# Two attention blocks on one core: transposes into eight PSUM banks by row chunks, image 0's norm inside the first product of weights, bias vectors as rows

## The chip, the core and the metric

The kernel runs on one core of a Trainium2 chip. The core has five engines that run side by side, each with its own queue of instructions in a fixed order: TensorE (PE) multiplies matrices and loads the stationary operand (PEld), VectorE (DVE), ScalarE (ACT) and GpSimd (POOL) work element by element, and SyncE (SP) issues most of the transfers between the chip's memory (DRAM) and the core's working memory. Engines wait for each other through semaphores. TensorE writes its results into PSUM, eight banks of 128 partitions by 512 fp32 numbers, from which DVE or ACT copy them out. The metric is the device time of one execution in microseconds (us). Before the change it is 3001.4 us, the median of 3 runs (2998.86 to 3006.32).

## The reference

The input is 8 images of 512 channels and 32 x 32 points, in fp32. Two attention blocks follow each other; everything is fp32.

```
# layer 0: group norm with 32 groups, 8 heads of 64 channels
h   = group_norm(x, 32 groups)
qkv = w_qkv @ h + b_qkv
att = softmax(q.T k / sqrt(64))            # 1024 x 1024 for each head
x   = x + w_proj @ (v @ att.T) + b_proj
# layer 1: group norm with 8 groups, one head of 512 channels
h = group_norm(x, 8 groups)
q, k, v = q_w @ h + q_b, k_w @ h + k_b, v_w @ h + v_b
att = softmax(q.T k / sqrt(512))
x = x + p_w @ (v @ att.T) + p_b
```

## The kernel before, in words

**What is computed.** The kernel folds layer 1's weights in pairs. Scores need only the product of the q and k weights (called m), and values followed by the projection need only the product of the p and v weights (called z). Both 512 x 512 products are made on the chip in a prologue, and so are the three vectors that come from biases carried through a weight matrix: `ubias`, `obias[1]` and `obias[0]`. A multiplication of an image by a weight matrix is done with seven products of half-sized blocks instead of eight (`wino`, L223). For that each weight matrix needs four sums of its quarters; `prepare` (L273) loads the quarters and makes the sums in four DVE instructions, and `keep` (L285) stores the seven blocks (1.8 MB) to DRAM, from where `load_weight` (L293) fetches them again whenever an image needs them. Three such weight tiles fit at a time, so the load of one waits until an earlier one has been stored or used.

**The prologue** (L554). It loads the raw k and q weights of layer 1 and image 0 and prepares v, q and k of layer 0. `natural` (L519) transposes a weight matrix, 16 blocks of 128 x 128 for each matrix, into PSUM, four blocks to a bank, and copies each bank out, even ones on DVE and odd ones on ACT. `product` (L532) multiplies, four outputs with four accumulating matmuls each. An fp32 matmul is two records in the profile, a transpose is one. `GroupNorm` (L88) has three parts: `stats` on DVE, `group_mean` (a small matmul and four small DVE instructions) and `affine` (a small matmul, DVE, a power on POOL, DVE), after which `apply` scales each of the four 128-channel chunks, in the prologue in turn on POOL and ACT. `bias_product` (L542) multiplies with the weights as the stationary operand and one bias column as the moving one. Then come the v, q and k products of image 0, the second product of weights (z), the other two bias vectors, and the norm of image 1. `acc_tile` (L187) gives one of two PSUM banks; three more pools (a, b, c) have two banks each.

**The attention of layer 0** (`attention0`, L395) works in 8 blocks for an image: a pair of heads by one half of the points. For each of 8 steps PE makes a score tile `sc` of two banks (three such tiles exist), ACT takes its exponential `e`, and DVE adds it to `total`. PE then multiplies the exponentials with v (`av`) and, in `reciprocals` (L366), adds `total` over partitions (the `sums` matmul). DVE takes the reciprocal (`rc`), SP writes it to DRAM as rows and reads it back to all partitions as `r`, and one block later DVE multiplies, `a <- av, r` (L435). Functions in `extra` are called inside the blocks: for image 0 they hold what `later` collected in the prologue (L594 to L598), that is the sums, the store and a weight load for p, m and z, in blocks 0, 1 and 2, and the norm of image 1.

**What sets the order.** A scheduling layer places instructions in each engine's queue by its own estimates, within the dependencies it sees. Instructions handed to `tc.keep_in_program_order` keep the order of the program among each other. Before the change that was so only for matmuls and transposes (L65 to L69); so the sums of weights could run on DVE much earlier than where the program names them.

## Time and profile before

The profile's execution has a span of 2998.6 us. All of the change lies in the first 150 us and in the first attention blocks.

| event | time, us |
| --- | --- |
| first transpose of the k weights | 4.9 |
| first product of weights on PE | 19.2 to 34.8 |
| small matmuls of ubias and image 0's norm | 34.6 to 39.5 |
| v, q and k products of image 0 | 42.8 to 117.1 |
| transposes of the v weights | 117.0 to 120.0 |
| second product of weights | 120.0 to 134.0 |
| bias matmuls of obias | 134.4 to 145.3 |
| first score matmul, first exponential | 145.3, 147.4 |
| sums of p, m, z on DVE begin | 73.9, 87.6, 145.4 |
| `sums` matmuls of the first five blocks | 162.1, 176.7, 191.9, 206.5, 222.4 |

The columns of a timeline line in what follows are: start, duration, engine, line of the kernel, operation, written tile and tiles read, shapes, how many such instructions were merged, and in brackets the time that the engine stood idle before it and what ended that. SPq is SP's queue, where a transfer has the time of its issue, not of its data. In the lines of stretches, each engine has its busy time and its number of instructions; the three last numbers are the clock that PE was granted (1.00 is full speed), the busy share of the 16 transfer engines and the GB/s that they moved. Busy time says little of what ends last; what counts is the idle time before an instruction on PE.

### The profile page before, as it was taken

The page shows a single profiled execution, that of the slowest core. Times are in us where ns is not written, and L with a number is a line of the kernel's source. Part 1 is how long each engine was busy: PE and PEld are TensorE (multiplying, and loading weights), DVE is VectorE, ACT ScalarE, POOL GpSimd, SP SyncE. Part 2 cuts the span into 40 slices and gives each one's busy share as a digit, 9 for nine tenths or more (in the row PEclk, how much of TensorE's full clock was granted, in tenths as well). Part 3 has the DMA queues.
Part 4 walks back from the last instruction along what each step waited for, and adds up shares of the span by engine and source line. Part 5 has one row for each costly group of instructions (what it writes and reads, how often), then busy time and mean ns, then how long its engine had stood idle before and what let it go on. Part 6 is the DMA issues. An engine that isn't in the chain of part 4 may idle for free.

```text
span 2998.6 us, 26895 instructions
## 1 busy us (share of the span) xinstructions
PE 2944.2 (98%) x10322; PEld 1409.5 (47%) x10322; DVE 1836.1 (61%) x2445; ACT 754.6 (25%) x925; POOL 112.8 (4%) x119
## 2 busy tenths in 40 slices
PE   7999999999999999999999999999999999999899
PEld 5535454354543545435453354534445354543345
DVE  4376565764667647575466754677546765557745
ACT  1153111421124111341114411143111431214220
POOL 0000000000000000000000000000000000000000
PEclk9999999999999999999999999999999999999899
DMA  7422314023140231402322133411324023030100
GB/s 258 166 80 80 138 60 172 19 92 130 59 169 18 107 142 51 150 27 100 144 101 96 47 115 113 145 46 46 130 105 168 19 76 140 33 144 19 39 0 37
DMA packets 78296, 283.56 MB, mean 95 GB/s; under 512 B 9360, under 2 KB 16336, under 8 KB 71632
## 3 DMA queue, kind: packets, MB, share of 16 engines
q1 hardware_dynamic: 77744, 281.61, 26.3%
q8 instruction: 83, 1.36, 0.2%
q14 instruction: 53, 0.43, 0.0%
q10 hardware_dynamic: 416, 0.16, 0.0%
HBM read 207.51 MB, written 74.22 MB: 94 GB/s over the span
## 4 chain that ended last, share of the span: by engine, by line
PE 84%; DVE 7%; issue 4%; DMA 3%; ACT 1%; SPq 0%; POOL 0%; DVEq 0%; ACTq 0%; POOLq 0%
PE sc L66 9%; PE av L66 8%; PE psb_av L66 5%; PE psb_sc L66 5%; DVE sum L417 5%; PE psa_av L66 4%; PE psc_av L66 4%; PE psc_sc L66 4%; PE psa_sc L66 4%; PE psb_z L66 3%; PE psb_q L66 3%; PE psb_v L66 3%; PE psb_g L66 3%; PE psb_k L66 3%; PE psb_p L66 2%
## 5 line engine op out<-in xcount | busy, mean ns | idle before, releaser
L413 ACT ACTIVATE e<-sc 128x1024 f32<-128x1024 f32 x512 | 476.4, 1051 | 582.7 <-PE sc L66 582.7
L417 DVE TENSOR_TENSOR sum<-sum,e 128x1024 f32<-128x1024 f32 x384 | 469.8, 1223 | 34.5 <-ACT e L413 0.8
L66 PE MATMUL sc<-q_again,k_again 64*128 64x512 f32 x1792 | 399.7, 596 | 0.0
L66 PE MATMUL av<-e,v_again 128*64 128x512 f32 x1792 | 396.9, 595 | 0.0
L66 PEld LDWEIGHTS sc<-q_again,k_again 64*128 64x128 f32 x1792 | 166.7, 186 | 212.2 <-ACT e L413 103.7
L66 PEld LDWEIGHTS av<-e,v_again 128*64 128x64 f32 x1792 | 123.7, 137 | 266.3 <-issue 254.2
L377 DVE RECIPROCAL rc<-sums 128x256 f32<-128x256 f32 x72 | 126.4, 1756 | 80.3 <-PE sums L66 47.7
L379 POOL TENSOR_TENSOR all_recs<-all_recs,rc 128x256 f32<-128x256 f32 x72 | 63.6, 883 | 1611.1 <-DVE rc L377 1611.1
L464 ACT ACTIVATE e<-e 128x512 f32<-128x512 f32 x96 | 60.3, 630 | 238.8 <-DVE e L463 238.8
L66 PE MATMUL psa_sc<-g,h 128*128 128x512 f32 x256 | 115.1, 592 | 0.0
L66 PE MATMUL psa_av<-e,z 128*128 128x512 f32 x256 | 113.2, 595 | 0.0
L415 DVE TENSOR_TENSOR sum<-e,e 128x1024 f32<-128x1024 f32 x64 | 78.4, 1225 | 48.9 <-ACT e L413 48.9
L136 ACT ACTIVATE h<-h,b,s 128x1024 f32<-128x1024 f32 x30 | 36.5, 1238 | 169.3 <-DMA h<-in_x 161.4
L66 PEld LDWEIGHTS psa_sc<-g,h 128*128 128x128 f32 x256 | 48.6, 190 | 61.2 <-issue 61.2
L66 PEld LDWEIGHTS psa_av<-e,z 128*128 128x128 f32 x256 | 48.0, 190 | 54.8 <-issue 50.6
L435 DVE TENSOR_TENSOR a<-av,r 128x512 f32<-128x512 f32 x64 | 43.9, 686 | 46.2 <-DMA r<-rows 46.2
L234 DVE TENSOR_TENSOR u_av<-psb_av,t_av 128x512 f32<-128x512 f32 x16 | 11.1, 691 | 93.1 <-PE psb_av L66 93.1
L66 PE MATMUL psb_p<-t_a,w_p 128*128 128x512 f32 x128 | 60.5, 615 | 5.2 <-DVE t_a L167 5.2
L66 PE MATMUL sums<-sum,ones 128*32 128x256 f32 x576 | 46.0, 391 | 18.1 <-DVE sum L417 17.9
L66 PE MATMUL psa_g<-h,w_m 128*128 128x512 f32 x128 | 60.0, 613 | 3.2 <-ACT h L136 3.2
L66 PE MATMUL sc<-q,k 64*128 64x512 f32 x256 | 59.2, 612 | 0.7 <-ACT e L413 0.7
L66 PE MATMUL psb_z<-w_z,t_h 128*128 128x256 f32 x256 | 58.4, 381 | 0.0
(281 smaller groups left out, 4159.1 us busy)
## 6 DMA issues: line engine op xcount, KB each, us to landing
x<-in_x SPq DMA_DIRECT2D x36, 512.0 KB
h<-in_x SPq DMA_DIRECT2D x32, 512.0 KB
r<-rows SPq DMA_DIRECT2D x128, 128.0 KB
out<-x SPq DMA_DIRECT2D x64, 256.0 KB
w_p<-sums_p SPq DMA_DIRECT2D x8, 1792.0 KB
spill<-v SPq DMA_DIRECT2D x28, 512.0 KB
w_m<-sums_m SPq DMA_DIRECT2D x8, 1792.0 KB
spill<-q SPq DMA_DIRECT2D x28, 512.0 KB
```

What stands on the lines that cost most here:

```text
L66: tc.keep_in_program_order(nc.tensor.matmul(*args, **kw))
L136: nc.scalar.activation(dst, src, AF.Identity, bias=b, scale=s)
L234: nc.vector.tensor_add(t[i], ps["b", i], t1[i])
L377: nc.vector.reciprocal(rc, sums)
L379: nc.gpsimd.tensor_tensor(all_recs, all_recs, rc, ALU.add)
L413: nc.scalar.activation(e, sc, AF.Exp, scale=(C // 8) ** -0.5)
L415: nc.vector.tensor_add(total, es[0], e)
L417: nc.vector.tensor_add(total, total, e)
L435: nc.vector.tensor_mul(a[hp][:, ts(tb, HT)], av, r)
L464: nc.scalar.activation(dst, dst, AF.Exp, scale=scale)
```

## The change

It rebuilds the prologue so that PE has less to wait for, in these parts:

- `raw` loads a weight matrix in four row chunks instead of two halves. `natural` goes through the chunks in its outer loop, so that a chunk is transposed as soon as it has landed, into four banks at once. The k and q weights together use all eight banks.
- The copies of transposed weights (DVE and ACT in turn), the statistics of image 0 and the sums of weights are kept in program order. The sums of v now stand after the first product.
- `group_mean` and `affine` of image 0 are called inside the first product, after its seventh and tenth matmul, and `apply` follows there.
- `bias_product` gives way to `bias_products`: a bias column is the stationary operand, the weights are the moving one, and the three results lie in one bank as rows at partitions 0, 32 and 64. They are copied out, written to DRAM as rows and read back as columns. All three are made after the second product.
- The raw weights for `obias[0]` are loaded before the second product.

```diff
--- before.py
+++ after.py
@@ -86,15 +86,17 @@
 
 
     class GroupNorm:
-        def __init__(self, layer, uid):
-            self.layer, self.uid = layer, uid
+        def __init__(self, layer, uid, pinned=False):
+            self.layer, self.uid, self.pinned = layer, uid, pinned
             self.mv = small.tile([P, KC, 2], F32, tag="mv", name=f"mv_{uid}")
             self.st = [None] * KC
 
         def half_stats(self, c, half, xh):
             if self.st[c] is None:
                 self.st[c] = small.tile([P, 2, 6], F32, tag="bnst", bufs=4, name=f"bnst_{self.uid}_{c}")
-            nc.vector.bn_stats(self.st[c][:, half, :], xh)
+            stats = nc.vector.bn_stats(self.st[c][:, half, :], xh)
+            if self.pinned:
+                tc.keep_in_program_order(stats)
 
         def end_stats(self, c):
             nc.vector.bn_aggr(self.mv[:, c, :], self.st[c])
@@ -278,7 +280,8 @@
                 nc.sync.dma_start(f[p], half(kh, mh))
             _, steps = left_sums(
                 [(f[1], f[7])], [(f[2], f[4])], (lambda j: f[5], lambda j: f[6], lambda j: f[3]),
-                nc.vector.tensor_add, nc.vector.tensor_sub,
+                lambda *a: tc.keep_in_program_order(nc.vector.tensor_add(*a)),
+                lambda *a: tc.keep_in_program_order(nc.vector.tensor_sub(*a)),
             )
             return t, steps
 
@@ -511,67 +514,86 @@
 
         def raw(n, i):
             ts_ = [pair_tile(f"raw{n}_{h}") for h in range(2)]
-            for h in range(2):
-                nc.sync.dma_start(ts_[h], w[i, ts(h, C // 2), :].rearrange("(kc p) o -> p kc o", p=P))
+            for kc in range(KC):
+                nc.sync.dma_start(ts_[kc // 2][:, kc % 2, :], w[i, ts(kc, P), :])
             return [ts_[kc // 2][:, kc % 2, :] for kc in range(KC)]
 
-
-        def natural(wt, nm):
+        def ps_tile(n, name):
+            return acc_tile(name) if n == "acc" else ps_pools["abc".index(n)].tile([P, HT], F32, tag="ps", name=name)
+
+        def spread(f, n):
+
+            for i in range(n):
+                f(i, nc.scalar.copy if i % 2 else nc.vector.tensor_copy)
+
+
+        def natural(wt, nm, banks):
             ts_ = [pair_tile(f"nat{nm}_{h}") for h in range(2)]
             t = [ts_[o // 2][:, o % 2, :] for o in range(KC)]
-            for o in range(KC):
-                pt = acc_tile(f"tr_w{nm}_{o}")
-                for kc in range(KC):
-                    transpose(pt[:, ts(kc, P)], wt[kc][:, ts(o, P)], ident)
-                if o % 2 == 0:
-                    nc.vector.tensor_copy(t[o], pt)
-                else:
-                    nc.scalar.copy(t[o], pt)
+            pt = [ps_tile(banks[o // 2], f"tr_w{nm}_{o}") for o in range(KC)]
+            for kc in range(KC):
+                for o in range(KC):
+                    transpose(pt[o][:, ts(kc, P)], wt[kc][:, ts(o, P)], ident)
+            spread(lambda o, copy: tc.keep_in_program_order(copy(t[o], pt[o])), KC)
             return t
 
-        def product(lhs, rhs, nm):
+        def product(lhs, rhs, nm, hooks=()):
+
+            hooks = dict(hooks)
             ts_ = [pair_tile(f"prod{nm}_{h}") for h in range(2)]
             for ic in range(KC):
-                ps = acc_tile(f"ps_w{nm}_{ic}")
+                ps = ps_tile("a", f"ps_w{nm}_{ic}")
                 for kc in range(KC):
                     matmul(ps, lhs[kc][:, ts(ic, P)], rhs[kc], start=(kc == 0), stop=(kc == KC - 1))
+                    if ic * KC + kc in hooks:
+                        hooks[ic * KC + kc]()
                 nc.scalar.copy(ts_[ic // 2][:, ic % 2, :], ps)
-            for h in range(2):
-                nc.sync.dma_start(products[nm][ts(h, C // 2), :].rearrange("(kc p) o -> p kc o", p=P), ts_[h])
-
-        def bias_product(dst, lhs, vec, add, nm):
-            for oc in range(KC):
-                ps = acc_tile(f"ps_b{nm}_{oc}")
-                for kc in range(KC):
-                    matmul(
-                        ps[:, 0:1], lhs[kc][:, ts(oc, P)], pcol(vec, kc), start=(kc == 0), stop=(kc == KC - 1)
+                if ic % 2:
+                    nc.sync.dma_start(
+                        products[nm][ts(ic // 2, C // 2), :].rearrange("(kc p) o -> p kc o", p=P), ts_[ic // 2]
                     )
-                if add is None:
-                    nc.vector.tensor_copy(dst[:, oc : oc + 1], ps[:, 0:1])
-                else:
-                    nc.vector.tensor_add(dst[:, oc : oc + 1], ps[:, 0:1], pcol(add, oc))
+
+        def bias_products(lhs):
+
+            n = len(lhs)
+            ps = acc_tile("ps_bias")
+            for kc in range(KC):
+                for i, (m, vec) in enumerate(lhs):
+                    matmul(ps[32 * i : 32 * i + 1, :], pcol(vec, kc), m[kc], start=(kc == 0), stop=(kc == KC - 1))
+            row = big_tile("bias_rows")
+            rows = dram.tile([n, C], F32, name="bias_rows_dram")
+            for i in range(n):
+                nc.vector.tensor_copy(row[32 * i : 32 * i + 1, :C], ps[32 * i : 32 * i + 1, :])
+            nc.sync.dma_start(rows, row[0 : 32 * n : 32, :C])
+            cols = const.tile([P, n, KC], F32, name="bias_cols")
+            for i in range(n):
+                nc.sync.dma_start(cols[:, i, :], rows[i].rearrange("(c p) -> p c", p=P))
+            return [cols[:, i, :] for i in range(n)]
 
         def prologue():
             raw_k = raw("k", 5)
             raw_q = raw("q", 4)
             h0 = [load_x(0, c, "h0") for c in range(KC)]
             first = {n: prepare(n) for n in "vqk"}
-            wk = natural(raw_k, "k")
-            wq = natural(raw_q, "q")
-            norm = GroupNorm(0, "0_0")
+            wk = natural(raw_k, "k", ("a", "b"))
+            wq = natural(raw_q, "q", ("c", "acc"))
+            norm = GroupNorm(0, "0_0", pinned=True)
             for c in range(KC):
                 norm.stats(c, h0[c])
+            hf, steps = image_factors(h0, "h0_0")
+
+            def normed():
+                norm.affine(acc_tile("gvar_0_0")[:, :KC])
+                for c in range(KC):
+                    norm.apply(nc.scalar if c % 2 else nc.gpsimd, h0[c], h0[c], c)
+
+            product(
+                wq, wk, "m", {6: lambda: norm.group_mean(acc_tile("gmean_0_0")[:, :KC]), 9: normed},
+            )
+            raw_v = raw("v", 6)
+            raw_p = raw("p", 7)
             for f in first["v"][1]:
                 f()
-            product(wq, wk, "m")
-            norm.group_mean(acc_tile("gmean_0_0")[:, :KC])
-            bias_product(ubias, wk, "bq1", None, "u")
-            norm.affine(acc_tile("gvar_0_0")[:, :KC])
-            for c in range(KC):
-                norm.apply(nc.scalar if c % 2 else nc.gpsimd, h0[c], h0[c], c)
-            raw_v = raw("v", 6)
-            raw_p = raw("p", 7)
-            hf, steps = image_factors(h0, "h0_0")
             background.extend(steps)
             for n in "qk":
                 background.extend(first[n][1])
@@ -587,10 +609,14 @@
             k = conv(weight_factors(first["k"][0]), hf, pcols("bk0"), "k0_0")
             finish()
             norm1.group_mean(acc_tile("gmean_0_1")[:, :KC])
-            product(natural(raw_v, "v"), raw_p, "z")
+            raw_p0 = raw("p0", 3)
+            wv = natural(raw_v, "v", "bc")
+            product(wv, raw_p, "z")
             norm1.affine(acc_tile("gvar_0_1")[:, :KC])
-            bias_product(obias[1], raw_p, "bv1", "bp1", "o")
-            bias_product(obias[0], raw("p0", 3), "bv0", "bp0", "o0")
+            bias = bias_products([(wk, "bq1"), (raw_p, "bv1"), (raw_p0, "bv0")])
+            nc.vector.tensor_copy(ubias, bias[0])
+            nc.vector.tensor_add(obias[1], bias[1], pcols("bp1"))
+            nc.vector.tensor_add(obias[0], bias[2], pcols("bp0"))
             later = []
             for n in "pmz":
                 t, steps = prepare(n)
```

## The prediction

> **What bounds the kernel now.** I read the page first: busy times and the chain that ended last.
>
> ```profile
> PE 2944.2 (98%) x10322; PEld 1409.5 (47%) x10322; DVE 1836.1 (61%) x2445; ACT 754.6 (25%) x925; POOL 112.8 (4%) x119
> PE 84%; DVE 7%; issue 4%; DMA 3%; ACT 1%; SPq 0%; POOL 0%; DVEq 0%; ACTq 0%; POOLq 0%
> ```
>
> TensorE (PE) fills the span, so time can only come from places where PE stands still or runs at a slow clock, and the change touches only the first 230 us. So I read the timeline there (start, duration, then the idle time before and what ended it).
>
> ```profile
> 10.62 1.29 DVE L97 BATCH_NORM_STATS2 bnst<-h 128x6 f32<-128x512 f32 x2 [9.34 <-DMA h<-in_x]
> 12.07 0.64 DVE L527 COPY natk<-tr_wk 128x512 f32<-128x512 f32 x1
> 12.76 1.97 PE L69 MATMUL tr_wk<-ident,rawk 128*128 128x128 f32 x8 [4.69 <-DVE natk L527]
> 19.20 15.59 PE L66 MATMUL ps_wm<-natk,natq 128*128 128x512 f32 x32
> 42.79 8.90 PE L66 MATMUL psa_v<-prepare_v,h 128*128 128x256 f32 x32 [3.26 <-POOL h L138]
> ```
>
> The first transposed bank waits for a copy that stands on VectorE (DVE) behind statistics of an image still in flight: PE idles 4.69 us, and the product starts at 19.20. It ends at 34.8; the first v matmul comes 8 us later, after small matmuls and the norm. Then the second half of the prologue, and two blocks of image 0's attention:
>
> ```profile
> 135.71 9.61 PE L66 MATMUL ps_bo<-par,rawp 128*128 128x1 f32 x56 [0.31 <-DVE obias L552]
> 139.79 2.49 ACT L136 ACTIVATE h<-h,b,s 128x1024 f32<-128x1024 f32 x2 [5.18 <-DMA h<-in_x]
> 162.08 0.64 PE L66 MATMUL sums<-sum,ones 128*32 128x256 f32 x8
> 165.30 0.39 SPq L297 DMA_DIRECT2D w_q<-sums_q  x1
> 166.32 1.15 SPq L391 DMA_DIRECT2D r<-rows  x2
> 173.85 0.69 DVE L435 TENSOR_TENSOR a<-av,r 128x512 f32<-128x512 f32 x1 [0.19 <-DMA r<-rows]
> 176.73 0.64 PE L66 MATMUL sums<-sum,ones 128*32 128x256 f32 x8
> 191.86 0.64 PE L66 MATMUL sums<-sum,ones 128*32 128x256 f32 x8 [0.41 <-DVE sum L417]
> ```
>
> Blocks take 176.73 - 162.08 = 14.65 us and PE hardly waits; but r, issued behind a weight load of 1.8 MB, landed 173.85 - 165.30 = 8.55 us after that load's issue, a microsecond or two before DVE would have held PE up. The Sync queue (SP) shows what a 1.8 MB store costs whoever waits for it, 82.91 - 77.18 = 5.73 us:
>
> ```profile
> 77.18 0.34 SPq L286 DMA_DIRECT2D sums_p<-prepare_p  x1
> 82.91 1.91 SPq L278 DMA_DIRECT2D prepare_m<-product_m  x4
> ```
>
> And the clock (the number before the last two) in stretches of 4 us:
>
> ```profile
> 134.00:138.00 4.00, 3.44 (x30) 3.27 (x30) 1.00 (x7) 0.59 (x1) 1.01 (x1) 1.00 0.93 290
> 142.00:146.00 4.00, 4.00 (x18) 3.73 (x20) 0.90 (x4) 0.28 (x1) 0.00 (x0) 0.50 1.02 411
> 150.00:154.00 4.00, 3.35 (x16) 0.98 (x12) 2.97 (x3) 4.00 (x6) 0.00 (x0) 1.00 0.98 389
> ```
>
> One-column matmuls leave PE at half clock.
>
> **What the Trainium skill says.** "TensorE: Matmul & The Clock Gate", Part 1: PE runs at half clock after an idle window of about 3.4 us and is released after as long a busy one. The trace agrees: ps_wm weights load 0.86 us apart from 19.2 to 22.6, then 0.43. Part 4 there: transposes don't count as busy; agrees, since 6 us of them precede that slow start. Part 3: matmuls on different 32-column tiles run side by side (three gave 2.38x); agrees, the eight sums matmuls on four tiles take 0.64 us, not eight times 0.215. "DMA: Bandwidth & Descriptors", Rules for kernel authors: a non-contiguous last dimension becomes one descriptor per element; no transfer of before shows it.
>
> **The change, part by part.**
>
> *Transposes and copies.* In the changed program's order the four DVE copies stand before all statistics, so the 4.69 us wait goes, and with a bank for each output nothing waits on PSUM. What remains is the transposes: 32, spaced (14.66 - 12.76)/8 = 0.2375 us at the cold clock, 7.6 us. Weights arrive faster than that (256 KB in 0.66 us at 390 GB/s, four transposes in 0.95). The first half of rawk landed at 4.87; a quarter I put at 4.2. So the last transpose ends at 11.8 and the product starts at 11.9, not 19.20: -7.3. If the clock did release, 10.6.
>
> *Norm within the product.* Two small matmuls move into it: 15.6 + 0.6, ending at 28.1. Is the norm in time? DVE's copies end at 12.5; four chunks of statistics at 1.48 (two of 0.64 and a 0.2 aggregate) end at 18.4; gmean's slot after seven products (3.4 of the time cold) is at 19.6. gvar follows at 22.2; from gvar to the applied h before took 41.54 - 39.17 = 2.4, so the factors are there at 24.5, and the halves by 26 and 27 on ScalarE (ACT) and GpSimd, ACT's held back prodm copy by 26.9. All lie beside the product. psa_v starts at 28.1 against 42.79: -14.7. It also starts warm: 32 at 0.216 (the next rows, 16 in 3.45) is 6.9, not 8.90: -2.0. DVE now makes prepare_k (4 x 0.68) ahead of w_v during the v product, and step 4 waits for w_v: +0.6. Image 1's loads on SP now wait for the store of prepare_k, until 45; its statistics end near 58 by the rate above, and the u_q add queued behind them is due at 66: nothing.
>
> *V transposes by chunk.* PE is at full clock here. All four copies come at the end and the last bank waits for a read of psc (117.82): +0.2. Sum at the end of the second product: -15.9.
>
> From here I write times on the clock of before (the product ends at 133.98) and subtract 15.9 at the end.
>
> *Bias rows.* Gone: 64 matmuls, 11.3 us to 145.25. (The 32 of ubias were counted above.) New: 24 of 512 columns on three tiles, 8 x 0.43 + 0.2 = 3.6, so scores start at 137.9. But ACT applies two chunks of image 1 before its first exponential, and the second's load now stands on SP behind the store of the rows, which waits for three DVE copies (3 x 0.69, until 139.9). It is issued at 140.9, and I put its landing at 144 (the first took 139.79 - 135.03 = 4.8 us behind 512 KB of product_z; this one has 256 KB ahead). The other two chunks stand behind three loads of 512 single elements. Their price is not shown: at the 14 ns a packet of the parameter loads' queue in the first 3 us (4.1% of 16 x 3 us over 144 packets) 1536 over 16 engines are 1.4 us; at the 162 ns of the average packet (26.3% of 16 spans over 77744) 15.6. I take 2, close to the low end: the 14 ns were packets of 192 to 512 bytes, and a packet of 4 bytes has less to move. Then chunks land at 147.2 and 148.4, exponentials at 0.95 until 155.4 (before 157.8), sums at 160.6: -1.5. So of the 7.4 that PE is earlier, ACT's wait takes back most; after 140.5 PE has used its three score tiles and stands.
>
> *Prepared weights.* In the built order prepare_p, m and z (2.72 each), before in idle DVE time at 74, 88 and 145, stand in blocks 0, 1 and 2 after the last sum. On SP follow: the store of it, rows, then a weight load that waits until that store has landed (same buffer), then r. So r lands 5.7 + 8.5 = 14.2 us after each prepare, and behind r on DVE stand a (0.7), the last sum (1.2) and the next prepare (2.7). That is a loop of 18.8 us against 14.65. Worked through: last sum 157.8, prepare_p 160.5, r 174.8; last sum 176.7, where PE arrived at 175.5; prepare_m 179.4, r 193.7, last sum 195.6 (PE at 191.6); prepare_z 198.3, r 212.6, fourth sums matmul at 214.5 against 206.52. With the -1.5 inside, +8.0. Two PE stalls of 4 us may cool the clock: between 0 and 1.7, I take 0.5. Later blocks keep their order.
>
> *At no cost.* The weights in eight loads instead of four (SP issues one in 0.48 us, the data take 0.66), the first product stored by halves (needed first at 83, by prepare_m), ubias made after the second product instead of before (first read after the attention), the fourth projection's weights loaded ahead of the second product (it has no reader until the bias rows).
>
> Sum: -15.9 + 8.0 + 0.5 = -7.4, so 3001.4 - 7.4 = 2994.0.
>
> **Rivals.** *The loop does not bind* (0.28): block 0's exponentials come early, or r isn't held by the load ahead of it. For: blocks of before have 1 to 2 us of slack. Against: 8.55 us is measured with just such a load. Loss 1.5: 2987.0. *Single elements are dear* (0.06): at 15.6 us instead of 2 everything behind image 1's load moves by 13.6, and PE cools: 2994.0 + 14 = 3008, slower than before. For: nothing bounds it; against: 14 ns a packet. *The norm comes late* (0.08): GpSimd's apply slowed by DVE beside it, or statistics waiting for a load, put PE idle for 3.5 us and cold for 2 more: 2999.5. The forecast has 0.58.
>
> **How the numbers follow.** The forecast's own error is some 3 us: the prologue's gain 13.5 to 17.5, the loss 5 to 13. With the first rival below and the third above, 2986.5 to 3001 leaves 2 in 10. More than 0.3% is 9 us (2992.4): four fifths of the first rival (0.22) and a fifth of the forecast (0.12) lie beyond it, 0.35; slower by 9 us needs the worst packets, 0.04; the rest 0.61.
>
> **What would show it.** Product start near 11.9, psa_v at 28 with no wait and 0.216 apart; second product's end near 118; scores stopping for ACT for some 5 us after three tiles; DVE's a waiting for r in blocks 1 to 3, PE's sums waiting for DVE by about 1, 4 and 4 us; SP's weight loads waiting for the stores. Wrong if those sums don't wait, or the single elements take over 5 us.

## The result and the profile after

The changed kernel takes 2987.4 us (median of 4 runs, 2987.3 to 2987.7), the kernel before beside it 3002.4 us (median of 4, 2998.9 to 3006.3): a ratio of 0.9950, 95% interval 0.9933 to 0.9967, so 15.0 us less where 7.4 were forecast. The kernel before spreads over 7 us, and in three later and larger sets of runs its median was 2998.6 to 2999.3 us, so the gain is nearer 13.6 us (2999.3 against the 2985.7 of the changed kernel in the same set). The profiled spans are 2985.4 and 2998.6 us.

First the page of the changed kernel, busy times and the chain that ended last:

```profile
PE 2931.7 (98%) x10250; PEld 1395.0 (47%) x10250; DVE 1839.2 (62%) x2439; ACT 754.5 (25%) x925; POOL 114.1 (4%) x119
PE 84%; DVE 7%; DMA 4%; issue 3%; ACT 1%; SPq 0%; DVEq 0%; POOL 0%; ACTq 0%; POOLq 0%
```

Nothing of the balance has moved, as was to be expected of a change within the first 230 us. The answer is in the timeline of PE up to 40 us:

```profile
3.76 3.83 PE L69 MATMUL tr_wk<-ident,rawk 128*128 128x128 f32 x16 [3.76 <-DMA rawk<-in_w]
7.38 2.92 PE L69 MATMUL tr_wq<-ident,rawq 128*128 128x128 f32 x16
10.75 6.28 PE L66 MATMUL ps_wm<-natk,natq 128*128 128x512 f32 x14 [0.46 <-DVE natq L537]
17.01 0.36 PE L66 MATMUL gmean<-mv,gm 128*128 128x4 f32 x2
17.22 2.82 PE L66 MATMUL ps_wm<-natk,natq 128*128 128x512 f32 x6
19.88 0.28 PE L66 MATMUL gvar<-dv,gm 128*128 128x4 f32 x2
20.02 5.40 PE L66 MATMUL ps_wm<-natk,natq 128*128 128x512 f32 x12
25.25 7.07 PE L66 MATMUL psa_v<-prepare_v,h 128*128 128x256 f32 x32
```

The wait of 4.69 us for a DVE copy is gone. The product starts at 10.75, not 19.20, and the v product follows it at 25.25 with no wait (42.79 before). The first 14 matmul records of the product take 6.28 us, 0.45 each: PE is at full clock from the first. The forecast had reckoned with half clock there.

Then the bias stage, on ACT and SP:

```profile
121.03 1.24 ACT L138 ACTIVATE h<-h,b,s 128x1024 f32<-128x1024 f32 x1 [4.99 <-DMA h<-in_x]
127.45 1.24 ACT L138 ACTIVATE h<-h,b,s 128x1024 f32<-128x1024 f32 x1 [5.18 <-DMA h<-in_x]
```
```profile
121.26 0.83 SPq L567 DMA_DIRECT2D bias_rows_dram<-bias_rows  x1
122.96 0.36 SPq L207 DMA_DIRECT2D h<-in_x  x1
123.43 1.47 SPq L570 DMA_DIRECT2D bias_cols<-bias_rows_dram  x3
```

Image 1's second chunk stands behind the store of the rows, is issued at 122.96 and lands 4.5 us later; ACT's first exponential waits for it, and PE stands 7.80 us with its three score tiles full. Last, the loop of blocks 1 to 3: PE's sums, DVE's a, and two rounds on SP.

```profile
160.30 0.64 PE L66 MATMUL sums<-sum,ones 128*32 128x256 f32 x8 [1.42 <-DVE sum L420]
178.80 0.64 PE L66 MATMUL sums<-sum,ones 128*32 128x256 f32 x8 [3.78 <-DVE sum L420]
197.22 0.64 PE L66 MATMUL sums<-sum,ones 128*32 128x256 f32 x8 [2.00 <-DVE sum L420]
```
```profile
158.42 0.69 DVE L438 TENSOR_TENSOR a<-av,r 128x512 f32<-128x512 f32 x1 [2.68 <-DMA r<-rows]
176.92 0.69 DVE L438 TENSOR_TENSOR a<-av,r 128x512 f32<-128x512 f32 x1 [3.70 <-DMA r<-rows]
195.35 0.69 DVE L438 TENSOR_TENSOR a<-av,r 128x512 f32<-128x512 f32 x1 [3.63 <-DMA r<-rows]
```
```profile
162.80 0.33 SPq L289 DMA_DIRECT2D sums_m<-prepare_m  x1
164.47 0.57 SPq L384 DMA_DIRECT2D rows<-rc  x1
168.42 0.32 SPq L300 DMA_DIRECT2D w_p<-sums_p  x1
168.79 1.10 SPq L394 DMA_DIRECT2D r<-rows  x2
```

The store goes out at 162.80, the weight load waits for it until 168.42 (5.6 us), r is behind the load and lands at 176.92 (8.1 us), 14.1 us after the store. The a's are 18.5 us apart; a block without this takes 14.65. A table of leads (after minus before, at the start of the same instruction) shows where the time is won and lost:

| instruction | before | after | lead |
| --- | --- | --- | --- |
| first product starts | 19.20 | 10.75 | -8.45 |
| v product starts | 42.79 | 25.25 | -17.54 |
| second product ends | 133.98 | 115.4 | -18.6 |
| sums, block 0 | 162.08 | 144.16 | -17.92 |
| sums, block 1 | 176.73 | 160.30 | -16.43 |
| sums, block 2 | 191.86 | 178.80 | -13.06 |
| sums, block 3 | 206.52 | 197.22 | -9.30 |
| sums, block 7 | 266.68 | 257.46 | -9.22 |
| last sums of the kernel | 2935.82 | 2922.70 | -13.12 |

So half of the prologue's gain is given back in blocks 1 to 3, and some 4 us are won later, in images whose code didn't change.

In the third of these blocks PE's clock has a part. After the stand of 3.78 us the scores take 8.83 us (7.14 in the block before), and the granted clock falls to half:

```profile
179.37 8.83 PE L66 MATMUL sc<-q,k 64*128 64x512 f32 x32
180.00:182.00 2.00, 2.00 (x8) 0.79 (x6) 2.00 (x4) 1.02 (x1) 0.00 (x0) 0.52 0.05 12
```

This cost nothing in the end: DVE sets when that block ends, and PE's wait at its end became shorter instead, 2.00 us.

### The profile page after: what moved, and what is told of

Its sections match the earlier page's. It is cut to its first block, busy times and chain, and to the rows that moved or that the text cites. A ratio compares the mean times of both kernels' runs of the same rounds, so it can differ in the third digit from the quotient of the medians.

```text
span 2985.4 us, 26766 instructions
## 1 busy us (share of the span) xinstructions
PE 2931.7 (98%) x10250; PEld 1395.0 (47%) x10250; DVE 1839.2 (62%) x2439; ACT 754.5 (25%) x925; POOL 114.1 (4%) x119
## 4 chain that ended last, share of the span: by engine, by line
PE 84%; DVE 7%; DMA 4%; issue 3%; ACT 1%; SPq 0%; DVEq 0%; POOL 0%; ACTq 0%; POOLq 0%
PE sc L66 9%; PE av L66 8%; PE psb_sc L66 6%; PE psb_av L66 6%; DVE sum L420 5%; PE psa_av L66 4%; PE psc_av L66 4%; PE psc_sc L66 4%; PE psa_sc L66 4%; PE psb_z L66 3%; PE psb_q L66 3%; PE psb_g L66 3%; PE psb_k L66 3%; PE psb_v L66 3%; DMA r<-rows 2%
```

## The experiments

Times are medians; ratios are to the kernel before on the same chip, whose median was 2998.6 to 2999.3 us in the three sets of runs. The changed kernel took 2985.7 us in the second set (the run "once more" below), and that is what "under the changed kernel" is counted from; these differences have no interval of their own, only those of the two ratios, and the four runs of the first set (sums freed, loads on GpSimd's queue, image 1 first, four banks) were on another chip.

### Does the loop cost the 8.7 us?

**The sums of p, m and z freed** from program order in the changed kernel:

```diff
-                lambda *a: tc.keep_in_program_order(nc.vector.tensor_add(*a)),
+                lambda *a: pin(nc.vector.tensor_add(*a)),     # and tensor_sub
+            pin = tc.keep_in_program_order if n in "vqk" else lambda i: i
```

> The changed kernel, with the weight sums of p, m and z no longer held in program order (those of v, q and k still are), so that they stand on DVE in the idle time of the prologue again. Theory (the loop: sums, store, weight load waiting for the store, r behind it, a, last sum): the 8.7 us that blocks 1 to 3 of image 0 lost against the kernel before come back, no sums matmul of blocks 1 to 3 waits more than 1.5 us for DVE, the difference to the kernel before at the eighth sums matmul is -17 to -18 instead of -9.2, and the time is 2978.7. Rival (the blocks lose time to something else, such as the state of the clock or image 1's chunks): 2987, within 1.5 us of the changed kernel.

Measured 2981.2 us, ratio 0.9939 (0.9925 to 0.9952), 4.4 under the changed kernel. Blocks 1 to 3 end 44.1 us after block 0 (before 44.4, changed kernel 53.1): the loop is gone and all of its loss comes back. But the first sums matmul came at 148.50 instead of 144.16, because the weight load w_v now stands on SP ahead of image 1's chunks. The theory holds for the blocks; the gain in all was half of what was expected.

**The kernel before with only these sums held in order**, as the change holds them:

```diff
-                nc.vector.tensor_add, nc.vector.tensor_sub,
+                lambda *a: pin(nc.vector.tensor_add(*a)),     # and tensor_sub
+            pin = tc.keep_in_program_order if n in "pmz" else lambda i: i
```

> The kernel before, with only one part of the change: the weight sums of p, m and z held in program order, so that they, their stores and the weight loads that wait for the stores stand in blocks 0, 1 and 2 of image 0's attention. Theory (the loop costs by itself 8 us, whatever the prologue does): block spacings of 16 to 18.5 us instead of 14.65 in blocks 1 to 3, the fourth sums matmul 7 to 10 us later than in the kernel before, and the time 8 us longer, a ratio of 1.0027. Rival (the loop binds only since the changed prologue brings the blocks so near to the loads of its end): no change, within 1.5 us.

Measured 3007.8 us, ratio 1.0030 (1.0018 to 1.0042): 8.5 us longer. Blocks 1 to 3 take 17.2, 18.6 and 18.3 us. The loop costs this by itself, whatever the prologue does. (The first sums matmul was also 1.8 us later; that was not followed up.)

### What in the loop makes r late?

**The three weight loads on GpSimd's queue**:

```diff
+                queue = nc.gpsimd if len(uses) >= 6 * B - 6 else nc.sync
-                nc.sync.dma_start(t, wdram[n])
+                queue.dma_start(t, wdram[n])
```

> The changed kernel, with the first three weight loads of image 0's attention issued from GpSimd's queue instead of the Sync queue, so that r no longer stands behind a load that waits for a store; the sums stay in blocks 0, 1 and 2 on DVE. Theory (r is late because it is queued behind the load that waits for the store): r lands some 3.5 us after its issue and a doesn't wait for more than 1.5 us; DVE's 2.7 us of sums alone cost 0 to 1.5 us in all, and the time is 2980. Rival (it is DVE's own time, 3 x 2.7 = 8.2 us of sums in blocks that have none to spare): the blocks stay at 16 to 18.5 us and the time stays within 1.5 us of 2987.

Measured 2991.8 us, ratio 0.9975 (0.9964 to 0.9985), 6 us over the changed kernel: neither came. DVE's and SP's timelines of that run:

```profile
158.72 0.69 DVE L439 TENSOR_TENSOR a<-av,r 128x512 f32<-128x512 f32 x1 [4.33 <-DMA r<-rows]
177.32 0.69 DVE L439 TENSOR_TENSOR a<-av,r 128x512 f32<-128x512 f32 x1 [7.52 <-DMA r<-rows]
```
```profile
163.10 0.33 SPq L289 DMA_DIRECT2D sums_m<-prepare_m  x1
164.77 0.57 SPq L385 DMA_DIRECT2D rows<-rc  x1
168.81 1.10 SPq L395 DMA_DIRECT2D r<-rows  x2
```

No load stands ahead of r on SP any more (GpSimd issues it at 169.23, after r), and still r is issued 4.0 us after the rows (1.7 in a quiet block) and lands 8.5 us after its issue. So my theory that the queue alone does it falls, and DVE's own time is not it either, since a waits for r. What is left is the transfers themselves: 1.8 MB out and 1.8 MB in share the 16 transfer engines with the 4 KB of rows and with r, two transfers of 128 KB. The Trainium skill, "DMA: Bandwidth & Descriptors", Queues, rings and completion order, says that each engine serves its queues in turn, a packet at a time; so a second queue brings r no free engine. The packets in this trace agree.

The load is 128 packets of 14 KB, r is 128 packets of 2 KB, so some eight of each for an engine if they are spread evenly. In the changed kernel, with one queue, r's packets begin only at 174.24, when the load's last ones start (174.65). Here they run among the load's, from 170.07 to 176.45, and a packet of the load takes 0.66 us. Behind the load or in turn with it, r is done when the load is. Its own packets are no slower than in a quiet block (0.09 us each, against 0.11 in the block at 533 us), so it is the turn that is waited for, not a slower memory. The rows stand behind the store in both runs: their packets begin at 167.92 and 168.21, just after the store's last (167.51 and 167.81). That the load waits for the store, finally, costs r little, as r is issued about as early after the rows with it (4.3 us) as without it (4.0).

**Stores and loads in different blocks**: the loads held back to blocks 3, 4 and 5 by a small GpSimd operation that reads the buffer to be written.

```diff
+            def hold(i, t):
+                nc.gpsimd.tensor_tensor(seen[:, i : i + 1], all_recs[:, 0, 0:1], t[:, 0, 0, 0:1], ALU.add)
-                later.append([lambda n=n, t=t: keep(n, t), load_weight])
+                later += [steps, [lambda n=n, t=t: keep(n, t)]]
+                held += [[lambda i=i, t=t: hold(i, t), load_weight], []]
```

> The changed kernel, with its sums and stores in blocks 0, 1 and 2 as they are, and the weight loads held back to blocks 3, 4 and 5 by one small GpSimd operation each, which reads the buffer that the load will write. Theory (r is late because a store and a load of 1.8 MB each, 9.4 us at 390 GB/s, run ahead of it on the same 16 DMA engines, whichever queue issues them): with the store alone r lands about 9 us after the sums instead of 14.7, a waits no more in blocks 1 to 3, those blocks take 14.7 to 15.5 us, blocks 3 to 5 lose at most 1.5 us each to the load, and the time is 6 to 8 us under the changed kernel's. Rival 1 (the store's wait alone binds): blocks 1 to 3 keep their 16 to 18.5 us. Rival 2 (DVE's 2.7 us of sums per block binds): the same blocks wait for DVE with no wait of a for r, and the gain is under 2 us.

Measured 2986.4 us, ratio 0.9950 (0.9937 to 0.9964): no gain. PE's waits in blocks 2, 4 and 6 show why.

```profile
175.16 0.64 PE L66 MATMUL sums<-sum,ones 128*32 128x256 f32 x8 [1.62 <-DVE sum L420]
208.54 1.08 PE L66 MATMUL sums<-sum,ones 128*32 128x256 f32 x8 [3.95 <-DVE sum L420]
242.85 0.64 PE L66 MATMUL sums<-sum,ones 128*32 128x256 f32 x8 [2.21 <-DVE sum L420]
```

Blocks 1 to 3 with the stores alone take 14.65, 16.34 and 14.71 us, 7.4 less than in the changed kernel; blocks 4 to 6 with the loads alone take 18.67, 17.38 and 16.93 us, 7.4 more. The first half of the theory holds, its bound of 1.5 us for a load does not. In blocks 4 and 6 DVE has a behind four of its seven sums, so an r that lands 8.8 us after its issue (194.16 to 203.00) is late for the three that follow. Block 5 has no wait at all; its 2.7 us are the clock's. In stretches of 2 us (the granted clock is the third number from the end):

```profile
206.00:208.00 2.00, 0.00 (x0) 0.00 (x0) 2.00 (x4) 0.00 (x0) 0.00 (x0) 0.84 0.00 0
208.00:210.00 2.00, 1.46 (x10) 0.65 (x12) 1.95 (x4) 0.00 (x0) 0.00 (x0) 0.50 0.00 0
214.00:216.00 2.00, 2.00 (x12) 1.04 (x10) 1.44 (x2) 1.68 (x3) 0.00 (x0) 0.95 0.80 272
```

PE's stand of 3.95 us ahead of block 4's sums takes it to half clock, and for some 6 us block 5's scores run at it (9.42 us instead of 7.14). So this wait of 4 us is paid for nearly twice.

### What holds up block 0?

**Image 1's loads ahead of the bias rows**:

```diff
+            early = [load_x(1, c, "h0") for c in range(KC)]
             bias = bias_products([(wk, "bq1"), (raw_p, "bv1"), (raw_p0, "bv0")])
-                h0 = [load_x(b + 1, c, "h0") for c in range(KC)]
+                h0 = early or [load_x(b + 1, c, "h0") for c in range(KC)]
```

> The changed kernel, with the four loads of image 1 issued ahead of the bias rows, so that they no longer stand behind the store of the rows and the loads of single elements. Theory: ACT's wait of 5.2 us for image 1's second chunk goes, the first exponential comes some 7 us earlier, the first sums matmul at 136 to 139 instead of 144.2, and as the loop of blocks 1 to 3 starts from that last sum, all of it reaches the end: 2980.5. Rival (what the blocks lose hangs on the stores and loads on the Sync queue, whose times do not move with image 1's chunks): the first sums matmul comes earlier, but the fourth stays at 197 and the time at 2987.

Measured 2976.7 us, ratio 0.9926 (0.9912 to 0.9939), 8.9 under the changed kernel. ACT applies three chunks at once, and the first exponential comes at 120.88 instead of 128.59:

```profile
117.46 3.51 ACT L138 ACTIVATE h<-h,b,s 128x1024 f32<-128x1024 f32 x3 [1.42 <-DVE b L133]
120.88 1.00 ACT L416 ACTIVATE e<-sc 128x1024 f32<-128x1024 f32 x1
```

The sums of block 0 start at 134.79 (9.4 earlier), those of block 3 at 188.83 (8.4 earlier): the loop is carried along, as the theory said. So the bias rows, 7.7 us less work on PE than the kernel before had there, brought nothing in the changed kernel only because of what their store held up on SP.

### What made the start early, and the clock fast?

**Four banks instead of eight** for the k and q transposes:

```diff
-            wq = natural(raw_q, "q", ("c", "acc"))
+            wq = natural(raw_q, "q", ("a", "b"))
```

> The changed kernel, with the transposes of q's weights put into the four banks that k's weights used, so that they wait for k's copies (a stand of some 0.7 us in the middle of the 32 transposes) as the kernel before did. Theory (transposes back to back do release the clock, a stand among them puts the release off by the time that was counted): the first product starts near 12.2, its first 2 to 4 matmuls are 0.86 us apart, its end is 2.5 to 4 us later than in the changed kernel, and the time is 2990.5. Rival (transposes have nothing to do with the clock): the product starts 1.5 us later and is at full clock from its first matmul, and the time is 2988.9.

Measured 2985.0 us, ratio 0.9952 (0.9938 to 0.9966): no difference. The copies of k were done when q's transposes came (the stand among them was 0.14 us, not the 0.7 assumed), and the product started at 10.73 at full clock. Eight banks are worth nothing here, and this run tells nothing of the clock.

**Neither copies nor statistics held in order**, banks and chunks as in the change:

```diff
-            spread(lambda o, copy: tc.keep_in_program_order(copy(t[o], pt[o])), KC)
+            spread(lambda o, copy: copy(t[o], pt[o]), KC)
-            norm = GroupNorm(0, "0_0", pinned=True)
+            norm = GroupNorm(0, "0_0", pinned=False)
```

> The changed kernel, with neither the copies of the transposed weights nor image 0's statistics held in program order, so that DVE's copies stand behind statistics of an image in flight as in the kernel before; banks and row chunks stay. Theory (the order on DVE is what made the start early, and PE cools if it stands long enough): the transposes end at 10.3 as in the changed kernel, the product starts at 15 to 15.5 instead of 10.75, its first four weight loads are 0.86 us apart after a stand of 5 us, and the time is 6.3 us longer, 2992. Rival 1 (banks and chunks alone give the early start): 10.75 again. Rival 2 (a stand of 5 us leaves the clock up): the start moves by 4.5 us, at 0.43 from the first matmul, 2990.2.

Measured 2990.3 us, ratio 0.9969 (0.9957 to 0.9981), 4.7 over the changed kernel. PE and its weight loads:

```profile
9.91 0.66 PE L69 MATMUL tr_wq<-ident,rawq 128*128 128x128 f32 x4 [0.59 <-DMA rawq<-in_w]
15.06 8.07 PE L66 MATMUL ps_wm<-natk,natq 128*128 128x512 f32 x14 [4.50 <-DVE natq L537]
```
```profile
16.08 0.33 PEld L66 LDWEIGHTS ps_wm<-natk,natq 128*128 128x128 f32 x1 [0.52 <-issue]
16.93 0.33 PEld L66 LDWEIGHTS ps_wm<-natk,natq 128*128 128x128 f32 x1 [0.52 <-issue]
17.79 0.33 PEld L66 LDWEIGHTS ps_wm<-natk,natq 128*128 128x128 f32 x1 [0.52 <-DVE bnst L97]
18.64 0.23 PEld L66 LDWEIGHTS ps_wm<-natk,natq 128*128 128x128 f32 x1 [0.52 <-issue]
19.11 0.19 PEld L66 LDWEIGHTS ps_wm<-natk,natq 128*128 128x128 f32 x1 [0.24 <-issue]
```

The product starts 4.3 us later, after a stand of 4.50 us, and its weight loads are 0.86 us apart for 3.6 us, then 0.43: the fast clock that 32 transposes had earned was lost in the stand (the granted clock is at half from 12 us on, 1.4 us into it) and had to be earned again. The v product starts at 31.15 (25.25). So DVE's order made the early start, and the theory holds to within 0.4 us at that point; the end kept 4.7 of the 5.9 us.

**The norm after the product**:

```diff
-                wq, wk, "m", {6: lambda: norm.group_mean(...), 9: normed},
+                wq, wk, "m",
             )
+            norm.group_mean(acc_tile("gmean_0_0")[:, :KC])
+            normed()
```

> The changed kernel, with image 0's norm after the first product of weights instead of within it. Theory (norm within the product is worth what PE would stand, plus the clock that the stand costs): the product ends near 24.7, the chain of two small matmuls, DVE, GpSimd and the applied chunks then takes 5.3 to 8 us as in the kernel before, so the v product starts at 30 to 32.5 instead of 25.25 and takes 8.9 us instead of 7.1; 8 us longer than the changed kernel, 2993.7. Rival (later waits of the prologue, for the loads of image 1 or for DVE's sums, take most of it up): under 4 us longer.

Measured 2991.6 us, ratio 0.9973 (0.9962 to 0.9983), 5.9 over the changed kernel. The product ends at 24.2; PE then waits 0.93 us for DVE and 3.64 us for GpSimd's chunk, and the v product starts at 29.27, 4.0 us later, and takes 9.92 us, 2.9 us longer at the cooled clock. Nearer to the theory than to the rival, 2 us smaller than expected.

### The late 4 us

**The changed kernel once more**, and **the kernel before with 14 transfers more** (the raw weights in quarters, as in the change, and four small loads of parameters that nothing reads):

```diff
-            for h in range(2):
-                nc.sync.dma_start(ts_[h], w[i, ts(h, C // 2), :].rearrange("(kc p) o -> p kc o", p=P))
+            for kc in range(KC):
+                nc.sync.dma_start(ts_[kc // 2][:, kc % 2, :], w[i, ts(kc, P), :])
...
+            for i in range(4):
+                nc.sync.dma_start(more_par[:, ts(i, 12)], params[:, ts(i, 12)])
```

> The changed kernel itself once more, as the measure for the other runs of this chip and for how far the kernel before spreads. Theory of the late 4 us (after image 0's attention the lead grows from 9.2 to 13.2 us only because r lands a microsecond later or earlier by chance): the lead at the eighth sums matmul is again 9 to 10 us, what is added to it later differs from that of the first run (13.2 at the end), and the ratio to the kernel before stays between 0.9933 and 0.9967. Rival (a lasting gain in every image): again 4 us are added after the eighth sums matmul, at the same blocks.

> The kernel before, with as many transfers on the Sync queue as the changed kernel has: each matrix of weights in four loads instead of two, and four small loads of parameters more, which nothing reads. Theory (the late 4 us come from where in the count of transfers the Sync queue's now and then slower issue falls: on a block of image 1 and one of image 4 that have no time to spare before, on others after): the lead at the eighth sums matmul stays within 1 us of the kernel before, the second and third blocks of image 1 lose 1.2 us less, and the time is 2 to 4 us shorter, a ratio of 0.9990. Rival (it is where the loads fall in time against each block): no change.

The changed kernel measured 2985.7 us, ratio 0.9955 (0.9941 to 0.9968); the other 2998.4 us, ratio 0.9995 (0.9987 to 1.0004), no difference. Both theories fell, chance and the count of transfers. The lead of the changed kernel's second profile again grows after image 0, from -9.10 to -13.68, and mostly at the same three blocks. Their length in us, from one sums matmul to the next:

| block | before | before, sums held | before, more transfers | after | after again | copies free |
| --- | --- | --- | --- | --- | --- | --- |
| image 1, third | 16.16 | 15.80 | 16.05 | 14.92 | 14.92 | 15.00 |
| image 3, fifth | 17.06 | 17.11 | 17.03 | 15.90 | 15.91 | 15.92 |
| image 4, seventh | 15.71 | 15.91 | 15.64 | 14.79 | 14.85 | 14.76 |

It isn't chance, then: it follows the program, in all fourteen profiles, three of them of the kernel before and its variants, and is worth 3.2 us. (The rest of the later images scatters as much: from the sums of block 7 to the last ones, these three blocks left out, the profiles take 2615.9 to 2620.2 us, in both families alike.) What one sees in the first of these blocks is SP's issue of the two halves of r, and a, in the kernel before and in the changed one:

```profile
542.63 2.27 SPq L391 DMA_DIRECT2D r<-rows  x2
547.43 0.69 DVE L435 TENSOR_TENSOR a<-av,r 128x512 f32<-128x512 f32 x1 [2.70 <-DMA r<-rows]
```
```profile
533.42 1.10 SPq L394 DMA_DIRECT2D r<-rows  x2
536.97 0.69 DVE L438 TENSOR_TENSOR a<-av,r 128x512 f32<-128x512 f32 x1 [1.46 <-DMA r<-rows]
548.52 2.17 SPq L394 DMA_DIRECT2D r<-rows  x2
```

In the kernel before the slow issue (2.27 instead of 1.10 us) falls on a block that has five sums behind a and so no time to spare; in the changed kernel it falls one block later (2.17 us), where r is in time all the same. The seventh block of image 4 has the same sign (1.91 us at 1690.8), the fifth of image 3 has not. What comes between is in the transfers of the trace, in a queue whose kind the profile gives as "instruction" (packets, MB, share of the engines' time in the changed kernel):

```profile
q8 instruction: 82, 1.34, 0.2%
```

These are packets of 16 KB, one every 36 us. In the kernel before, one starts at 543.27, one at 1299.87 and one at 1691.30, each between the issue of r and its landing in one of the three blocks, and r lands 4.80, 4.58 and 4.29 us after its issue. In the changed kernel none comes in these three waits, and r takes 3.55, 3.47 and 3.32 us. The kernel before in the block of image 3, where SP's issue has its usual length:

```profile
1297.56 1.10 SPq L391 DMA_DIRECT2D r<-rows  x2
1302.14 0.69 DVE L435 TENSOR_TENSOR a<-av,r 128x512 f32<-128x512 f32 x1 [2.58 <-DMA r<-rows]
```

After 300 us, behind image 0's bulk transfers, a waits for r 313 times in the fourteen profiles. In 18 of these r takes over 4 us, and all 18 have such a packet between issue and landing; 271 have none, and there r never takes more than 3.95 us. The slow issues go with the packets too: every one over 1.4 us there has one that starts in it or at most 0.15 us before. So the late gain goes with where these packets fall, which is luck for this change. What moves them no run shows. In both kernels one packet comes for about 250 of PE's records, and the change takes 72 matmul records and 72 weight loads away ahead of the attention, while 14 more transfers left the packets in the same blocks; so I take them to be fetches of PE's instructions, which is not shown.

### A version that beats both

**Sums freed and image 1 first**, the two edits above together:

> The changed kernel with both edits that gained: the sums of p, m and z not held in program order, and image 1's loads ahead of the bias rows. Theory (the two losses are independent: the loop of blocks 1 to 3 costs 8.7 us, image 1's chunks 8 us at the first sums matmul): first sums matmul at 135 to 137, eighth at 238.5 to 241, 17 us under the changed kernel's time. Rival (the weight loads that then stand around the end of the prologue come between image 1's chunks or the first r and take it back, as 4.3 us of the first sums matmul were taken back when only the sums were freed): 10 us under.

Measured 2971.8 us, ratio 0.9911 (0.9896 to 0.9926), 13.8 under the changed kernel: half way between theory and rival. Sums of block 0 at 135.75 and of block 7 at 244.70, 12.9 earlier than in the second profile of the changed kernel. What is missing lies in blocks 1 and 2, which take 17.97 and 16.30 us: the load w_q waits on SP for the store of z, and r of block 0 comes behind it; after the stand of 3.25 us that follows, the scores of block 2 take 8.62 us instead of 7.14.

**Besides, each weight load behind the a of block 0, 1 or 2**, so behind that block's r:

```diff
                         nc.vector.tensor_mul(a[hp][:, ts(tb, HT)], av, r)
+                        if behind_a:   # the small operation that reads a and the buffer, then load_weight
+                            behind_a.pop(0)(a[hp][:, tb * HT : tb * HT + 1])
```

> The changed kernel with the sums of p, m and z not held in program order, image 1's loads ahead of the bias rows, and the three weight loads each behind one small GpSimd operation that reads the a of blocks 0, 1 and 2, so that each starts once that block's r has landed and is over before the next. Theory (what is left of the loss, 4.5 us at the eighth sums matmul, comes from bulk transfers ahead of r in the queue): first sums matmul at 135 to 136, blocks of 14.65 to 15 us, eighth at 240 to 241, and the time 4 us under the version without the third edit (2971.8): 2967.8. Rival (the load slows the next block's r just as much from behind): 2971 to 2973.

Measured 2972.2 us, ratio 0.9911 (0.9897 to 0.9924): the rival. Block 1 is back at 14.65 us, but blocks 2 and 4 take 16.9 and 17.2. SP of that run:

```profile
148.62 0.34 SPq L302 DMA_DIRECT2D w_v<-sums_v  x1
152.37 0.57 SPq L386 DMA_DIRECT2D rows<-rc  x1
155.74 1.10 SPq L396 DMA_DIRECT2D r<-rows  x2
```

The load, 3.75 us old when the rows go out, still slows them: 3.37 us from rows to r instead of 1.7. A load of 1.8 MB after a block's r reaches into the next block's. Both versions are 27 us (0.9%) under the kernel before.

## Why the prediction was right in direction and too small

**Transposes and copies: right, and mis-sized.** Forecast: the product from 11.9, the first 3.4 us of it cold. Measured 10.75, near the value that I gave for "if the clock did release" (10.6). The step that failed is the reading that transposes don't count as busy for the clock. The Trainium skill says so ("TensorE: Matmul & The Clock Gate", Part 4), and I found the trace of before to agree. Here, with fp32, the measurement decides against it: in all ten profiles of the changed prologue in which the product followed the 32 transposes within 0.6 us, it was at full clock from its first matmul, and the transposes themselves went from 0.24 us each (16 of k in 3.83) to 0.13 to 0.18 on average (16 of q in 2.10 to 2.92). Nor does the kernel before agree, when it is profiled again. In the run with its sums held, which has the same prologue up to there, the last eight transposes take 1.09 us and all of the product is at full clock; in the profile that I had read they took 1.97 us, and the product 15.59.

```profile
17.25 1.09 PE L69 MATMUL tr_wq<-ident,rawq 128*128 128x128 f32 x8 [0.68 <-ACT natq L531]
18.69 14.00 PE L66 MATMUL ps_wm<-natk,natq 128*128 128x512 f32 x32 [0.35 <-DVE natq L529]
```

So what I took for a rule was where the clock happened to turn in one execution. A stand of 4.50 us undoes the release (copies free), with 3.6 us of product at half clock after it; that agrees with Part 1 there, which has some 3.4 us for either turn of a window that runs on its own. Worth 1.15 us of start, 0.44 of them because the first chunk landed at 3.76 and not at 4.2, and 1.7 of product; how much of the 1.7 the kernel before lacks varies, as its product took 15.59, 14.72 and 14.00 us in three profiles (itself, with more transfers, with its sums held).

**Norm within the product: right.** v product without a wait, 32 matmuls in 7.07 us (forecast 6.9), w_v's wait 0.53 (0.6). To the end of the second product -18.6 us where -15.9 was forecast, nearly all of the difference from the clock and the earlier chunk.

**Bias rows: mechanism right, term mis-sized by 2.1 us.** 24 matmuls in 3.6 us as forecast, and ACT's wait for image 1's chunk behind the store of rows came as described. But the chunk landed 4.5 us after its issue, not 3.1, and block 0 lost 0.6 us where 1.5 were to be gained. Single-element loads: three loads of 512 elements were issued from 123.43 and the columns were read at 127.63. The trace has 1536 packets of 4 bytes for them, 9 ns each, nearly all within 2 us: near the low end taken (whose 144 packets were of 192 and 4 bytes, not of 192 to 512). The skill's remark on one descriptor for each element ("DMA: Bandwidth & Descriptors", Rules for kernel authors) named a real form, but at this size the price was small.

**Prepared weights: right.** From block 0 to block 3 the changed kernel gave back 8.6 us (-17.92 to -9.30), forecast 9.5; a loop of 18.5 us, forecast 18.8; waits of PE 1.4, 3.8 and 2.0 us, forecast about 1, 4 and 4. The runs widened the reason and left the number: r is late because 3.6 MB pass the same engines around it, and a place in another queue than the load's doesn't free it. The 0.5 us for a cooler clock had the clock right and the cost wrong: PE was at half clock after the stand of 3.78 us, for 1.7 us of scores, but the third wait took it up, 2.0 us and not 4.

**What no step had: the late 4 us.** I took the blocks after the eighth to be the same in both kernels. They have the same instructions, but three of them are 0.9 to 1.2 us shorter, because no instruction packet falls between the issue and the landing of their r any more. That was luck. The sum of the profiles closes: -7.4 - 2.65 (clock and first chunk) + 2.1 (chunk) - 0.9 (loop) - 0.5 (stalls) - 3.9 (late) = -13.3, and the profiles differ by -13.2. That the forecast was too small has two main reasons, then, the clock and the instruction packets.

**The rivals.** That the loop doesn't bind fell (held alone in the kernel before it costs 8.5 us), though its time, 2987.0, was nearest, for other reasons; dear single elements and a late norm did not show.

## What to carry to other kernels

A gain on the critical engine lasts only as far as the next queue allows: half of what the prologue won was lost in a few blocks whose small transfer had to share the transfer engines with bulk stores and loads that the same change had moved there. Read from the instruction order of the changed program which bulk transfers now lie around a small one that someone waits for, and put them where nobody waits; giving the load another queue did not help. Keeping an order by hand is worth it for the few instructions that need it (copies ahead of statistics: 4.7 us) and can cost as much for those swept along (sums of weights: 8.5 us). And a gain of a few us in code that didn't change may only be luck with what now falls beside it, as here the instruction packets.

## What the runs showed of the hardware beyond that

- A run of 32 fp32 transposes brings PE to full clock; stands of 0.23 and 0.56 us among them (two of the runs) did not prevent it.
- How long PE stands does not alone decide whether the clock falls. After stands of 3.07 us (loads on GpSimd's queue) and 3.78 us (changed kernel) it went to half; with one of 3.58 us (image 1 first) it stayed up. The stretches at half clock in image 0 of the changed kernel last 10.2 and 3.4 us.
- 4 KB written and r read back take 1.7 us from the rows to r's issue and 3.5 us to land in a quiet block; with a store or load of 1.8 MB under way 3.0 to 4.8 us from the rows to r's issue, and with a load of 1.8 MB 7.5 to 9.3 us to land, whether SP or GpSimd issued the load.
- SP's issue of two transfers, 1.10 us as a rule, now and then takes 1.4 to 2.3 us; after 300 us in the fourteen profiles, each of these has an instruction packet of 16 KB in it or just before it. Three of the slow ones are the same in both profiles of the changed kernel (near 150, 262 and 548 us), two come in the second alone.
